# A gated cross-attention block with a top-8 expert mix: the first chunk taken by row tiles, the router centred once, gates folded into evictions, Newton's step on GpSimd, and a new order for the end

## The chip, the cores and the metric

The kernel runs on one core of a Trainium2 chip. The metric is the device time of one execution in microseconds (us). Beside the times of several runs there is one profiled execution, from which all rows below come. A core has five engines with instruction streams of their own: TensorE (PE in the profile; its weight loads are PEld), VectorE (DVE), ScalarE (ACT), GpSimd (POOL) and SyncE (SP, which only issues DMA transfers; ACT issues some too). An engine works through its stream in order and waits on semaphores for what others produce. TensorE writes to PSUM[...]; DVE and ACT carry results from there to SBUF, which all engines share.

## The reference, cut to what matters

The input `x` is 8 batches of 512 rows by 2048 columns, float32; `c` has the same shape. Per batch:

```python
h   = layernorm(x)                       # over the 2048 columns of each row
q   = Wq @ h + bq ; k = Wk @ h + bk      # 256 x 2048, in patches of 128 columns
val = Wv @ c + bv
s   = q_head.T @ k_head / sqrt(32)       # 8 heads, 128 x 128 in each patch, masked
o   = gelu(softmax(s) @ val_head)
x1  = x + tanh(g_xattn) * (Wo @ o + bo) * mask
h2  = layernorm(x1)
p   = softmax(h2 @ Wr.T + br)            # 64 experts for each row of 2048 columns
w   = the 8 largest of p, zeros elsewhere
out = x1 + tanh(g_ffn) * (h2 * sum(w) + w @ Eb)
```

Wq, Wk and Wv are 256 x 512, Wo is 512 x 256, Wr and Eb are 64 x 2048. A row of a batch (512 of them, four tiles of 128) is a token for the router.

## The kernel before, in words

**Tiles and steps.** A batch is cut into 4 chunks of 512 columns, so there are 32 chunks (`ch` 0 to 31; the last is `z`), each 512 rows in four row tiles (`m` 0 to 3). A step `g` of the main loop is half a chunk, two patches of 128 columns: 64 steps, of which 62 are in the loop (L755 to L940) and the last two, with all that is left over, in an end written out by hand (L943 to L1050). A batch is 8 steps.

**What a step does.** `scores(g)` puts q·k into the four score banks of PSUM (sc0 to sc3); `maxima` (L459, DVE), `exps` (L468, ACT, 16 instructions) and `divide` (L476 DVE, L477 POOL) make the softmax; `turn` (L491, PE) and `turned` (L497, ACT) transpose it, one step later; `weigh` (L510) multiplies it with the values, two steps later. For the next chunk `queries_and_keys` (L361 to L405) computes half of q and k by seven block products in place of eight, with sums of inputs and outputs on DVE and POOL: the sum u4 (L392, POOL) is read by ks (L400, DVE), which frees a PSUM buffer. These products, the values (L415) and others share two PSUM buffers ("mm"); transposes share two others ("tr"). `attend` (PE L539, DVE L545, POOL L548) projects a finished chunk and adds it to x in `xr`; `statistics2` (L558), `turn_x` (L563, L565) and `logits` (L574) feed the second norm and the router. When a batch is done, `gather` (L598), `choose` (L605), `choose_exps`, `select` (L630) and `turn_weights` (L653) find the eight experts of each token, and 12 steps later `scale_x` (L674 POOL, in the end L672 ACT too) and `mix` (PE L685, DVE L689, output DMA L690) make the output in eight parts of two row tiles each.

**The norms.** Statistics are collected in pieces by DVE (L264, L558). `aggregate` merges them (L244), adds epsilon (L245, DVE) and takes a power on POOL (L246); `refine` (L251 to L255) is one Newton step for the inverse square root, on DVE. For the first norm of the next batch both are called in the step with `g % 8 == 5`: `aggregate` ahead of the first divide, `refine` behind `queries_and_keys`. For the second norm they are called in the step `fin == 2` (the third step of the next batch). `norm` (L273) then applies it; in the loop ACT does (L285), in the prologue DVE and POOL (L290).

**The prologue** (L698 to L748). The loads of the first batch's x are spread over the SP and ACT queues. PE first computes values(0,0), (0,1) and (1,0), then the first chunk's q and k (pf, L344) in two halves of two row tiles each, as `norm` delivers them; sums of weights are on POOL (L208 to L210).

**The router's mean.** Logits are taken of x1 without its norm. `choose` puts the norm in afterwards, with the column sums of the router's weights (`rwsum`, made in `router_sums` by 32 PE passes at g = 1, L747), by two DVE operations for each row tile (L609, L613). The two tanh gates scale Wo (L936, POOL, g = 1) and the expert biases (L938, POOL, g = 3).

**Order.** Nothing is reordered by a scheduler: each engine executes its instructions in the order in which the program names them. A DMA goes out when its engine comes to it; eight completion slots are used in turn over the program's DMAs.

Of the kernel before, what the change touches and what calls it, by code (L numbers as in the profile page):

```python
# [16 lines left out]
P = 128  # L17
# [18 lines left out]
def flamingo_gated_kernel(  # L36
# [81 lines left out]
    def load_mask(ch):  # L118
        t = work.tile([P, CW], F32, tag="mk", name=f"mk_{ch}", bufs=4)
        nc.sync.dma_start(t, masks[ch // NCH, :, columns(ch)].to_broadcast([P, CW]))  # L120
        mks[ch] = t
# [33 lines left out]
    load_first_x(0)  # L155
    load_cx(0, 1)
    nc.scalar.dma_start(bv_sb, bv.partition_broadcast(P))
    load_first_x(1)

    def load_projections():  # L160
        nc.sync.dma_start(wq_sb, wqT.rearrange("(m p) e -> p m e", p=P))
        nc.scalar.dma_start(wk_sb, wkT.rearrange("(m p) e -> p m e", p=P))
        load_first_x(2)
        load_first_x(3)
        with nc.allow_non_contiguous_dma(reason="short bias vectors onto partitions"):
            nc.scalar.dma_start(bq_sb, bq.rearrange("(t p) -> p t", p=P))
            nc.scalar.dma_start(bk_sb, bk.rearrange("(t p) -> p t", p=P))
            nc.scalar.dma_start(bo_sb, bo.rearrange("(t p) -> p t", p=P))
        nc.scalar.dma_start(gates[:, 0:1], g_xattn.partition_broadcast(P))
        nc.scalar.dma_start(gates[:, 1:2], g_ffn.partition_broadcast(P))  # L170
        nc.scalar.dma_start(rb_sb, rb.partition_broadcast(P))
        load_mask(0)
# [16 lines left out]
    nc.vector.memset(ones, 1.0)  # L189
# [17 lines left out]
    def weight_sums():  # L207
        nc.gpsimd.tensor_tensor(ws1, w21, w22, ALU.add)  # L208
        nc.gpsimd.tensor_tensor(ws2, ws1, w11, ALU.subtract)
        nc.gpsimd.tensor_tensor(ws4, w12, ws2, ALU.subtract)  # L210
# [20 lines left out]
    def aggregate(st, n, name, m0=0, m1=NM):  # L231
# [9 lines left out]
        mv, v, r = lns[name][:3]  # L241
# [3 lines left out]
        nc.vector.tensor_scalar(v[:, ms], mv[:, ms, 1], EPS, None, ALU.add)  # L245
        nc.gpsimd.tensor_tensor(r[:, ms], v[:, ms], half[:, ms], ALU.pow)  # L246

    def refine(name, m0=0, m1=NM):
        mv, v, r, y, nmean = lns[name]
        ms = slice(m0, m1)  # L250
        nc.vector.tensor_tensor(y[:, ms], r[:, ms], r[:, ms], ALU.mult)  # L251
        nc.vector.tensor_tensor(y[:, ms], y[:, ms], v[:, ms], ALU.mult)
        nc.vector.tensor_scalar(y[:, ms], y[:, ms], -0.5, 1.5, ALU.mult, ALU.add)
        nc.vector.tensor_tensor(r[:, ms], r[:, ms], y[:, ms], ALU.mult)
        nc.vector.tensor_scalar(nmean[:, ms], mv[:, ms, 0], -1.0, None, ALU.mult)  # L255
        if m1 == NM:
            del lns[name]
        return nmean, r
# [14 lines left out]
    def norm(ch, ms=range(NM), engines=None):  # L273
        nmean, rs = ln1[ch // NCH]
        if ch // NCH not in nmrs and not engines:
            nmr = small.tile([P, NM], F32, tag="nmr", name=f"nmr_{ch}")
            nc.vector.tensor_tensor(nmr, nmean, rs, ALU.mult)
            nmrs[ch // NCH] = nmr
# [3 lines left out]
        for m in ms:  # L282
            e = engines[m % 2] if engines else nc.scalar
            if e is nc.scalar:
                e.activation(  # L285
                    xn[ch][:, m, :], source[:, m, :], AF.Identity,
                    bias=nmrs[ch // NCH][:, m : m + 1], scale=rs[:, m : m + 1],
                )
                continue
            e.tensor_scalar(  # L290
# [45 lines left out]
    def first_queries_and_keys():  # L336
# [4 lines left out]
        for m0 in range(0, NM, 2):  # L341
            for i, (w, e, pt) in enumerate(parts):
# [5 lines left out]
                if m0 == 0:  # L348
                    continue
# [359 lines left out]
    for i in range(NPP):  # L709
        values(0, 1, i)  # L710
# [374 lines left out]
```

## Time and profile before

| | |
|---|---|
| median of 3 runs | 1371.03 us (1370.95 to 1373.88) |
| the profiled execution | 1372.72 us |
| its span (first to last instruction) | 1370.9 us |
| PE busy, and idle in the span | 1317.3 us, 53.6 us |
| DVE, ACT, POOL busy | 912.9, 832.0, 778.0 us |
| first product of chunk 0 (pf) begins, ends | 26.67 us, 40.57 us |
| one batch of the steady part | 161.96 us |
| first scores of the end | 1274.65 us |
| first add of the last batch's output | 1355.79 us |

A group of the profile's rows reads: line, engine, operation, output <- input, partitions x elements, count, busy time, mean ns. A row of the timeline reads: start, duration, engine, line, operation, output <- input, count, and in brackets the idle time before it and what ended that. A row by stretches gives its length, the busy time (and number of instructions) of PE, PEld, DVE, ACT and POOL, then the granted clock of TensorE (1.00 is full), the DMA engines' share and GB/s. Engine names with a q (SPq, ACTq) are issues of DMAs.

### The profile page before, as it was taken

How to read it: one execution, taken by the hardware profiler on the slowest of the kernel's cores; microseconds unless marked ns; L12 is line 12 of the kernel's file. 1: busy time of each engine (PE TensorE's matmuls, PEld its weight loads, DVE VectorE, ACT ScalarE, POOL GpSimd, SP SyncE). 2: the span in 40 equal slices, each digit the busy share in tenths (PEclk: the TensorE clock that was granted, in tenths of full speed). 3: DMA queues.
4: the chain of work that ended last, by engine and by line, in shares of the span. 5: the costliest groups of instructions: out<-in, count | busy, mean ns of one | idle time of the engine just before them, and what ended most of it. 6: DMA issues, size and time to landing. Idle time of an engine off the chain costs nothing.

```text
span 1370.9 us, 26555 instructions
## 1 busy us (share of the span) xinstructions
PE 1317.3 (96%) x9816; PEld 961.0 (70%) x9816; DVE 912.9 (67%) x1981; ACT 832.0 (61%) x2837; POOL 778.0 (57%) x656
## 2 busy tenths in 40 slices
PE   7899999999999999999999999999999999999984
PEld 4686777777777677767777777776777777776642
DVE  5556665676676766786667767677677766567536
ACT  0565666757656666747665675666675566575533
POOL 3456565555566655557555566655556665556452
PEclk9999999999999999999999999999999999999997
DMA  8432323424434433444442444343444343232213
GB/s 276 133 102 71 101 65 129 131 70 156 153 131 139 161 100 133 147 140 141 151 137 96 146 162 141 129 158 97 139 147 161 109 131 105 75 122 78 104 67 123
DMA packets 109666, 173.32 MB, mean 126 GB/s; under 512 B 9185, under 2 KB 43617, under 8 KB 109409
## 3 DMA queue, kind: packets, MB, share of 16 engines
q1 hardware_dynamic: 105680, 168.32, 37.5%
q10 hardware_dynamic: 3856, 3.32, 0.7%
q8 instruction: 77, 1.26, 0.4%
q14 instruction: 53, 0.43, 0.1%
HBM read 138.06 MB, written 33.55 MB: 125 GB/s over the span
## 4 chain that ended last, share of the span: by engine, by line
PE 84%; DVE 11%; POOL 2%; DMA 1%; issue 1%; ACT 0%; DVEq 0%; POOLq 0%; ACTq 0%
PE qk L378 27%; PE po L539 16%; PE pv L415 13%; PE pt L491 7%; PE pl L574 4%; PE pb L685 4%; PE pa L510 4%; PE sc L447 3%; PE px L563 3%; DVE st L558 3%; DVE st L264 2%; PE sc L438 1%; PE pf L344 1%; DMA cx<-in_ctx 1%; DVE ks L405 1%
## 5 line engine op out<-in xcount | busy, mean ns | idle before, releaser
L477 POOL TENSOR_TENSOR at<-at,rsum 128x1024 f32<-128x1024 f32 x128 | 244.3, 1909 | 289.9 <-DVE rsum L476 255.4
L468 ACT ACTIVATE at<-sc,nmx 128x128 f32<-128x128 f32 x1024 | 365.7, 415 | 16.1 <-DVE nmx L459 16.1
L468 ACT ACTIVATION_READ_ACCUMULATOR at<-sc,nmx 128x1 f32 x1024 | 260.1, 254 | 0.0
L415 PE MATMUL pv<-wv_sb,cx 128*128 128x256 f32 x1024 | 242.6, 386 | 10.2 <-DMA cx<-in_ctx 10.2
L539 PE MATMUL po<-o,wo_sb 128*128 128x512 f32 x512 | 233.8, 599 | 0.0
L415 PEld LDWEIGHTS pv<-wv_sb,cx 128*128 128x128 f32 x1024 | 191.4, 194 | 33.8 <-DMA cx<-in_ctx 10.6
L548 POOL TENSOR_TENSOR xr<-t,xr 128x512 f32<-128x512 f32 x128 | 165.9, 1296 | 79.9 <-DVE t L545 79.5
L497 ACT COPY atT<-pt 128x512 f32<-128x512 f32 x256 | 151.1, 623 | 60.4 <-PE pt L491 60.3
L520 ACT COPY o<-pa 128x512 f32<-128x512 f32 x64 | 37.6, 587 | 243.9 <-PE pa L510 243.9
L459 DVE TENSOR_REDUCE nmx<-sc 128x4 f32<-128x512 f32 x256 | 158.7, 681 | 16.7 <-PE sc L447 16.6
L545 DVE SCALAR_TENSOR_TENSOR t<-po,bo_sb,mk 128x512 f32<-128x512 f32 x128 | 96.1, 751 | 109.5 <-PE po L539 104.6
L491 PEld LDWEIGHTS pt<-ident,at 128*128 128x128 f32 x1024 | 123.3, 142 | 61.8 <-issue 41.5
L539 PEld LDWEIGHTS po<-o,wo_sb 128*128 128x128 f32 x512 | 94.3, 190 | 100.4 <-issue 93.9
L565 ACT COPY x1T<-px 128x512 f32<-128x512 f32 x128 | 74.9, 587 | 139.3 <-PE px L563 136.2
L491 PE MATMUL pt<-ident,at 128*128 128x128 f32 x1024 | 152.2, 277 | 5.8 <-POOL at L477 5.3
L378 PE MATMUL qk<-xt,wq_sb 128*128 128x256 f32 x496 | 129.6, 384 | 4.0 <-DVE u L386 3.9
L378 PE MATMUL qk<-xn,ws 128*128 128x256 f32 x496 | 128.6, 382 | 0.0
L378 PE MATMUL qk<-xn,wk_sb 128*128 128x256 f32 x496 | 127.5, 380 | 0.0
L689 DVE TENSOR_TENSOR xr<-pb,xr 128x512 f32<-128x512 f32 x128 | 81.8, 683 | 36.4 <-PE pb L685 33.4
L674 POOL TENSOR_SCALAR xr<-xr,xa,xd 128x512 f32<-128x512 f32 x120 | 94.4, 798 | 18.6 <-DVE xa L650 18.6
L378 PEld LDWEIGHTS qk<-xn,ws 128*128 128x128 f32 x496 | 94.7, 191 | 13.0
L378 PEld LDWEIGHTS qk<-xn,wk_sb 128*128 128x128 f32 x496 | 89.4, 190 | 9.7
(108 smaller groups left out, 2016.3 us busy)
## 6 DMA issues: line engine op xcount, KB each, us to landing
out_dram<-xr SPq DMA_DIRECT2D x64, 512.0 KB, 3.4
cx<-in_ctx SPq DMA_DIRECT2D x63, 512.0 KB, 5.2
raw<-in_x SPq DMA_DIRECT2D x112, 256.0 KB, 3.4
xn<-in_x SPq DMA_DIRECT2D x28, 1024.0 KB, 7.3
xr<-in_x SPq DMA_DIRECT2D x28, 1024.0 KB, 7.8
mk<-in_mask_Bx1x_ff SPq DMA_DIRECT2D x32, 256.0 KB, 5.3
xr<-in_x SPq DMA_DIRECT2D x8, 256.0 KB, 6.4
xr<-in_x ACTq DMA_DIRECT2D x8, 256.0 KB, 6.9
```

Of the source, the lines that this page charges most:

```text
L378: nc.tensor.matmul(out_, w_[:, j, es], xb[:, j, :], start=(j == 0), stop=(j == NM // 2 - 1))
L415: nc.tensor.matmul(pv[:, i, :], cx[:, m, i * W : (i + 1) * W], wv_sb[:, m, :], start=(m == 0), stop=(m == NM - 1),)
L459: nc.vector.tensor_reduce(p["nmx"][:, r, :, :], p["sc"][r], AX.X, ALU.max, negate=True)
L468: nc.scalar.activation(p["at"][i][:, h, :], p["sc"][r][:, i, e, :], AF.Exp, bias=p["nmx"][:, r, i, e : e + 1], accum_out=p["rsum"][:, i, h ...
L477: (engine or nc.gpsimd).tensor_tensor(p["at"][i], p["at"][i], rs[:, :, None].to_broadcast([P, H, W]), ALU.mult)
L491: nc.tensor.transpose(pt[:, r, :], p["at"][i][:, e * HR + r, :], ident)
L497: nc.scalar.copy(p["atT"][i][:, e * HR : (e + 1) * HR, :], p.pop("pt"))
L539: nc.tensor.matmul(po[:, cs], wo_sb[:, e, m * P : (m + 1) * P], os_[ch][:, e, cs], start=(e == 0), stop=(e == NE - 1),)
L545: nc.vector.scalar_tensor_tensor(t[:, cs], po[:, cs], bo_sb[:, m : m + 1], mks[ch][:, cs], ALU.add, ALU.mult)
L548: nc.gpsimd.tensor_tensor(xc, t[:, cs], xc, ALU.add)
L674: nc.gpsimd.tensor_scalar(xc, xc, a, d, ALU.mult, ALU.add)
L689: nc.vector.tensor_tensor(xc, pb[i], xc, ALU.add)
```

## The change

1. **First chunk.** The x rows are loaded first, with Wq, Wk and cx(0,1) ahead of rows 1 to 3; mask 0, the short vectors, the gates and the router bias follow on ACT's queue; cx(1,0) and mask 1 stand behind them on SP's. The prologue runs over single row tiles: statistics, `aggregate`, the norm of chunks 0 and 1 (all on ACT), and that tile's four products; values(0,1) come after the first tile, values(1,0) in step 0. The sums of weights go from POOL to DVE, behind the last tile.
2. **Norms.** `refine` is merged into `aggregate`, all small operations behind the merge are on POOL, and so is the product of mean and inverse deviation (`shares_of_mean`). In the steps with `g % 8 == 5` the whole stands behind the first divide and ahead of `queries_and_keys`.
3. **Router.** In place of `router_sums` and the first of `choose`'s two operations, `centre_router` (at the end of g = 3) subtracts from the router's weights their mean over the columns.
4. **Gates.** Wo is scaled on ACT; the expert biases are no longer scaled, but the transposed weights are, as they are carried out of PSUM.
5. **Select.** The four small operations on `a` and `d` go from DVE to POOL, and the sum they need stands earlier.
6. **First statistics of batch 1.** The extra pieces in the steps 0 to 2 are read at the end of the step instead of behind the maxima.
7. **The end** has a new order: the last scores earlier, `scale_x` in pairs, parts 4 to 7 of the last but one batch's mix later, the adds of `attend(z)` on DVE, the last chunk turned by row tiles (`turn_last`), mixes held in PSUM until their adds, rows split between ACT and POOL in the last `scale_x`, the last two outputs split over two queues.

```diff
+    nc.sync.dma_start(wq_sb, wqT.rearrange("(m p) e -> p m e", p=P))
+    nc.scalar.dma_start(wk_sb, wkT.rearrange("(m p) e -> p m e", p=P))
     load_cx(0, 1)
+    for m in range(1, NM):
+        load_first_x(m)
+    load_mask(0, nc.scalar)
+    with nc.allow_non_contiguous_dma(reason="short bias vectors onto partitions"):
+        nc.scalar.dma_start(bq_sb, bq.rearrange("(t p) -> p t", p=P))
+        nc.scalar.dma_start(bk_sb, bk.rearrange("(t p) -> p t", p=P))
+        nc.scalar.dma_start(bo_sb, bo.rearrange("(t p) -> p t", p=P))
     nc.scalar.dma_start(bv_sb, bv.partition_broadcast(P))
...
+    nc.scalar.dma_start(gates[:, 0:1], g_xattn.partition_broadcast(P))
+    nc.scalar.dma_start(gates[:, 1:2], g_ffn.partition_broadcast(P))
+    nc.scalar.dma_start(rb_sb, rb.partition_broadcast(P))
+    load_cx(1, 0)
+    load_mask(1)
...
-    nc.vector.memset(ones, 1.0)
+    nc.vector.memset(ones, 1.0 / S)
...
     def weight_sums():
-        nc.gpsimd.tensor_tensor(ws1, w21, w22, ALU.add)
...
+        nc.vector.tensor_tensor(ws1, w21, w22, ALU.add)
...
-        nc.vector.tensor_scalar(v[:, ms], mv[:, ms, 1], EPS, None, ALU.add)
-        nc.gpsimd.tensor_tensor(r[:, ms], v[:, ms], half[:, ms], ALU.pow)
-
-    def refine(name, m0=0, m1=NM):
...
+        e = nc.gpsimd
+        e.tensor_scalar(v[:, ms], mv[:, ms, 1], EPS, None, ALU.add)
+        e.tensor_tensor(r[:, ms], v[:, ms], half[:, ms], ALU.pow)
+        e.tensor_tensor(y[:, ms], r[:, ms], r[:, ms], ALU.mult)
+        e.tensor_tensor(y[:, ms], y[:, ms], v[:, ms], ALU.mult)
+        e.tensor_scalar(y[:, ms], y[:, ms], -0.5, 1.5, ALU.mult, ALU.add)
+        e.tensor_tensor(r[:, ms], r[:, ms], y[:, ms], ALU.mult)
+        e.tensor_scalar(nmean[:, ms], mv[:, ms, 0], -1.0, None, ALU.mult)
...
+    def shares_of_mean(b, ms=slice(0, NM)):
...
+        nc.gpsimd.tensor_tensor(nmrs[b][:, ms], nmean[:, ms], rs[:, ms], ALU.mult)
...
-        for m in range(NM):
-            nc.vector.scalar_tensor_tensor(
-                lg[:, m, :], rwsum, nmean[:, m : m + 1], lg[:, m, :], ALU.mult, ALU.add
-            )
...
+        a = small.tile([P, NM], F32, tag="xa", name=f"xa_{b}")
+        d = small.tile([P, NM], F32, tag="xd", name=f"xd_{b}")
+        nc.vector.tensor_reduce(a, top, AX.X, ALU.add)
...
+        nc.gpsimd.tensor_tensor(a, a, t["rs"], ALU.mult)
+        nc.gpsimd.tensor_scalar_mul(a, a, tgates[:, 1:2])
+        nc.gpsimd.tensor_tensor(d, a, t["nmean"], ALU.mult)
+        nc.gpsimd.tensor_scalar(a, a, 1.0, None, ALU.add)
...
-        nc.scalar.copy(wT, pw)
+
+        nc.scalar.activation(wT, pw, AF.Copy, scale=tgates[:, 1:2])
...
+    new_queries_and_keys(0)
+    for m in range(NM):
+        for j in range(NCH):
+            statistics(0, m, j, xr[j][:, m, :])
+        ln1[0] = aggregate(st1[0], S // 512, "1_0", m, m + 1)
+        shares_of_mean(0, slice(m, m + 1))
+        norm(0, (m,))
+        norm(1, (m,))
+        if m == NM - 1:
+            mask(0)
+        next(projections)
+        if m == 0:
+            for i in range(NPP):
+                values(0, 1, i)
+    st1.pop(0)
+    weight_sums()
+    values_out(0, 0)
+    values_out(0, 1)
+    for k in range(3):
+        sums_of_x(1, k)
+    weight_sums_in_place()
...
+    def centre_router():
+
+        nc.vector.tensor_reduce(rwsum, rw_sb.rearrange("p k e -> p e k"), AX.X, ALU.add)
         pr = ps_tr.tile([P, E], F32, tag="tr", name="pr")
...
+        nc.tensor.matmul(pr, ones, rwsum, start=True, stop=True)
+        nc.vector.tensor_tensor(
+            rw_sb, rw_sb, pr[:, None, :].to_broadcast([P, NK, E]), ALU.subtract
+        )
...
-            if fin == 5 and b4 + 2 < B:
-                aggregate(st1.pop(b4 + 2), S // 512, f"1_{b4 + 2}")
...
             divide(g, 0)
+            b1 = g // SPB + 1
+            if g % SPB == 5 and b1 < B:
+                ln1[b1] = aggregate(st1.pop(b1), S // 512, f"1_{b1}")
+                shares_of_mean(b1)
...
-            router_sums()
-            nc.gpsimd.tensor_scalar_mul(wo_sb, wo_sb, tgates[:, 0:1])
+            nc.scalar.activation(wo_sb, wo_sb, AF.Copy, scale=tgates[:, 0:1])
         if g == 3:
-            nc.gpsimd.tensor_scalar_mul(eb_sb, eb_sb, tgates[:, 1:2])
+            centre_router()
+        read_x(len(pieces))
...
+    scores(g)
+    weigh(h0 - 1)
+    weighed(h0 - 1)
+    maxima(g, (0, 1))
+    maxima(g, (2, 3))
+    mix(b - 1, 2)
+    for k in (4, 5):
+        scale_x(b - 1, k)
+    turn_x(z - 2, 0)
...
+    for m in (0, 1):
+        attend(z, m, engine=nc.vector, tag=t_raw)
         statistics2(z - 1, m)
         statistics2(z, m)
...
+    turn_last(0)
+    turn_last(1)
+    logits(z - 1)
+    logits_out(z - 1)
+    turn_last(2)
+    mix(b - 1, 5)
+    turn_last(3)
...
+    mix(b - 1, 6, hold=True)
     choose(b)
     choose_exps(b)
+    added(b - 1, 6)
...
     for k in range(2 * NCH):
-        scale_x(b, k, k % 2 == 0)
+        scale_x(b, k, (0,), nc.scalar)
+        scale_x(b, k, (1,))
     for k in range(2 * NCH):
-        mix(b, k)
+        mix(b, k, hold=True)
+        added(b, k, (nc.sync, nc.scalar) if k >= 2 * NCH - 2 else (nc.sync,))
```

## The prediction

> **What bounds the kernel now.** I read the page first (engine shares and the 40 slices), then busy time by stretches, then the timeline wherever TensorE (PE) has idle time, then the groups of GpSimd (POOL).
>
> ```profile
> PE 1317.3 (96%) x9816; PEld 961.0 (70%) x9816; DVE 912.9 (67%) x1981; ACT 832.0 (61%) x2837; POOL 778.0 (57%) x656
> PE   7899999999999999999999999999999999999984
> PEclk9999999999999999999999999999999999999997
> ```
>
> PE is busy 96% of the span; the other engines have a third to spare. The lower digits of PE stand at the two ends only, and there alone the granted clock falls. The same by stretches (length, then busy time with instruction count of PE, PEld, DVE, ACT, POOL, then granted clock, DMA share, GB/s):
>
> ```profile
> 0.00:27.00 27.00, 16.84 (x49) 13.45 (x50) 14.99 (x43) 1.28 (x1) 6.25 (x11) 0.87 0.94 298
> 27.00:41.00 14.00, 13.89 (x35) 5.80 (x34) 5.31 (x17) 3.50 (x6) 8.66 (x8) 1.00 0.83 216
> 290.00:1250.00 960.00, 955.04 (x7244) 703.15 (x7240) 664.78 (x1429) 618.31 (x2117) 577.55 (x488) 1.00 0.41 133
> 1274.60:1325.30 50.70, 43.81 (x355) 26.95 (x353) 22.29 (x37) 25.45 (x87) 24.19 (x23) 0.93 0.29 105
> 1325.30:1370.90 45.60, 28.30 (x108) 14.09 (x106) 26.80 (x71) 13.81 (x28) 13.25 (x14) 0.81 0.28 104
> ```
>
> From 290 to 1250 us PE idles 5.0 us in 960: work taken from another engine there is worth almost nothing, and work put in front of PE costs in full. Of the 53.6 us that PE idles (1370.9 − 1317.3), 10.2 lie in the first 27 us, 24.2 in the last 96.3. So the change is decided at the ends, and by whether it breaks the middle.
>
> **Start: +6.5 us.** Before, the products of the first chunk (pf, L344) run from 26.67 to 40.57 us. The start of the timeline, PE beside the queues:
>
> ```profile
> 20.29 6.55 PE L415 MATMUL pv<-wv_sb,cx 128*128 128x256 f32 x16 [3.78 <-DMA cx<-in_ctx]
> 21.92 0.42 ACTq L168 DMA_DIRECT2D bo_sb<-in_L_xattn_bo  x1
> 23.45 0.41 ACTq L171 DMA_DIRECT2D rb_sb<-in_L_ffn_router_bias  x1
> 23.89 1.28 ACT L285 ACT_TABLE_LOAD   x1 [23.89 <-DMA xr<-in_x]
> ```
>
> The bo issue waits until 21.92: wq, the issue eight places earlier in program order, left at 13.50 and took 8.4 us to land. The other waits of these two queues that I followed fit the same spacing of eight. Now all norms of chunk 0 are on ScalarE (ACT), and 18 issues stand on its queue ahead of the first. The last, rb, stands eight behind the new place of cx(1,0) on SyncE's queue (SP). That in turn stands eight behind a piece of row 2 that I put down as landed at 16.6 (the DMAs move 367 GB/s from 5 to 20 us, and only what lies ahead of it counts). 16.6 + 8.2 for cx(1,0) under load = 24.8 for rb; + .41 issue, + 1.28 table load, + .75 for one ACT norm = 27.25 for the first operand of PE. The four rows' products are 4 × 3.43 = 13.7, and values(0,1), now between them, 3.46. PE has then been idle since about 13 us. [...] the row, 16 pv matmuls at 6.55 after 3.78 idle where the 16 at 622.51 take 3.62, loses 2.9 to 3.1. I take 2.6. End of pf: 27.25 + 17.2 + 2.6 = 47.05, against 40.57: +6.5 (+4 to +8.5: whether the wait resolves at 22.5 or 26.5). Hidden: x rows landing earlier, since ACT isn't there to use them.
>
> **First steps: −1.3 us in sum.** After pf, DVE has ks, three weight sums (.68 each, from POOL), two vT (.69), w21 and bo before the maxima, which come 5.1 us after pf (before: 2.0); scores cover part, and values(1,0), 16 matmuls of 3.46 us moved out of the prologue, stand against the router sums' 32 matmuls (pr, 3.68) that go. With the clock's dip from this stall I take +.7 (0 to +3). The extra row statistics go ahead of later maxima in g = 2 and 3: +.7. The new centring at g = 3 puts a DVE reduce over 128 × 1024 (1.3: twice the .68 of 128 × 512), one matmul and a DVE subtract over as much (1.2) in front of DVE's next maxima: +1.5 (0 to +3); the four DVE operations saved per batch (.87) have PE as their cover and count nothing. Against it stands a stall that goes. GpSimd's eb_sb scaling (5.44 us, L938) held the adds that PE turns next:
>
> ```profile
> 115.67 0.33 PE L563 MATMUL px<-ident,xr 128*128 128x128 f32 x1 [1.39 <-POOL xr L548]
> 117.08 0.33 PE L563 MATMUL px<-ident,xr 128*128 128x128 f32 x1 [1.08 <-POOL xr L548]
> 118.11 1.82 PE L378 MATMUL qk<-xn,ws 128*128 128x256 f32 x4
> ```
>
> Waits of 1.39 + 1.08 and, behind them, three groups at low clock (1.82 and two more, against their full-clock 1.03; together 1.76): −4.2. It becomes a scale inside an eviction, at nothing (ACT, the same copy). The wo_sb scaling goes from POOL (2.85) to ACT at g = 1, hidden under ACT's idle third. Sum .7 + .7 + 1.5 − 4.2 = −1.3.
>
> **Middle: +2.5 us.** Newton's step, five DVE operations of .16 per batch and norm, becomes a chain of eight on POOL, each waiting for the one before. Once per batch (g mod 8 = 5, seven times) it stands between divide(g,0) and the u4 add of queries_and_keys. Rows there: what POOL does now, and who waits for u4.
>
> ```profile
> L246 POOL TENSOR_TENSOR rs<-v,half 128x4 f32<-128x4 f32 x15 | 15.4, 1024 | 75.2 <-DVE v L245 75.2
> L392 POOL TENSOR_TENSOR u<-u,s 128x256 f32<-128x256 f32 x62 | 45.0, 726 | 30.2 <-DVE s L391 30.1
> 621.50 0.73 POOL L392 TENSOR_TENSOR u<-u,s 128x256 f32<-128x256 f32 x1
> 622.26 0.48 DVE L400 SCALAR_TENSOR_TENSOR ks<-qk,bk_sb,u 128x256 f32<-128x256 f32 x1 [0.81 <-POOL u L392]
> ```
>
> No small POOL arithmetic is in the trace. POOL's adds cost .73 for 256 columns and 1.28 for 512 (L308), so a straight line leaves .2 at none: 7 × (.2 + .09 for the wait) + 1.02 for pow = 3.0. POOL runs its scale_x and divide earlier, since pow no longer stands ahead of them, and u4 begins at 621.85 instead of 621.50. The ks after it holds a PSUM buffer that PE's next product wants: .35 × 7 = 2.5. Bounds: 0 (the step in PE's slack) and 10 (each operation .16 dearer). At LN2 (fin = 2) the same chain has 3.8 us before the next divide; it is hidden. The four operations of select (a, d) end at 607.9 by the same price, against 608.09 for their user: hidden, barely.
>
> **End: −14.3 us.** The end, as the timeline has it before:
>
> ```profile
> 1304.26 6.04 POOL L674 TENSOR_SCALAR xr<-xr,xa,xd 128x512 f32<-128x512 f32 x8
> 1312.21 1.97 PE L491 MATMUL pt<-ident,at 128*128 128x128 f32 x8 [4.53 <-POOL at L477]
> 1343.84 1.97 PE L598 MATMUL pg<-ident,lgT 128*128 128x64 f32 x8 [2.58 <-DVE lgT L588]
> 1352.48 0.69 PE L659 MATMUL pw<-ident,rest 128*128 128x128 f32 x2 [6.67 <-DVE rest L642]
> 1355.79 1.29 DVE L689 TENSOR_TENSOR xr<-pb,xr 128x512 f32<-128x512 f32 x2 [2.41 <-PE pb L685]
> ```
>
> From the first scores of the end (1274.65, called 0): last scores +20, the eight scalings delay divide(g,1) and PE 4.5, first output projection of the last chunk (attend(z,0)) +50.6, gather +69.2, first output add +81.1, end +96.25. After: scores(g) come ahead of four turns, weigh and turn_x, at +11; attend(z,0) at +39.9: three of the six mixes ahead of it move behind (1.2 of PE each, 3.6), the 4.5 goes, and the waits of scores for DVE's t (2.6 in this stretch by the view of waits) go with their buffers' new order. From there to gather it was 18.6, of which PE worked 15.8 and idled 2.8, almost all before gather, for lgT behind the statistics on DVE. Now the statistics lie between the adds: 15.8 + 1.2 for one mix moved in + .7 for DVE's lgT add = 17.7, gather +57.6. From gather to first add it was 11.9; off come the four DVE operations of choose (.9), five of select (.8), and .9 because pg (1.97 for eight small matmuls) finds PE warm: first add +66.9. From first add to end it was 15.1, four megabytes of output at 371 to 389 GB/s, and stays: end +82.0, −14.3 (−10: one stall like the old one; −19: the adds of the held mixes early and nothing waiting). The last outputs, split over two queues, save nothing while the DMAs are full.
>
> **Sum.** +6.5 − 1.3 + 2.5 − 14.3 = −6.6. The profiled execution took 1372.7 us (span 1370.9 and 1.8 around it), so 1366.1; the median of the runs is 1.7 lower, so 1364.4 there. I predict 1364.
>
> **Rivals.** A: the ACT queue isn't held. For it: the spacing of eight is inferred from waits that fit it. Norms then follow the rows (the last at about 30 us, pf end 34), 12.5 earlier than in my sum: 1352. B, slower: small POOL operations are dear. At .29 with its wait each one the stall is .35; at .6 the chain takes 5.2, the stall 2.5 plus as much for PE at lower clock behind it, 7 × 5 = 35 less what slack recovers, say half: +17 in place of 2.5: 1379. It decides from about .48 per operation, where the stall of 1.7 each time eats what is in hand. For it: nothing of that size is in the trace; against it: the straight line, and a POOL pow on 128 × 2 at .72 and on 128 × 4 at 1.02, more than half of it by element. C: the end's new order stalls elsewhere (one row of statistics on DVE ahead of an add, PSUM buffers shared by held mixes) and gives 8 only: 1364 + 6.3 = 1370 to 1371, no change. That the change does nothing isn't possible: the order of all engines moves.
>
> **How the numbers follow.** Mine .64 (own range 1357 to 1370, from the bounds above taken as half independent), A .13, B .12, C .11. Runs of this kernel tell apart 0.2%, 2.7 us, so faster is below 1368.3 and slower above 1373.8. Faster: .58 + .13 + .03 of C = .74; same: .06 + .06 = .12; slower: B .12 + .02 of C = .14. The range 1354 to 1375 leaves out most of A below and most of B above.
>
> **What would show it.** Right: first pf at 27 to 28 us behind ACT's rb issue, pf end near 47; no PE wait at 115 to 121; PE stalls under .5 at u4 of g = 5, 13, 21; POOL's small operations at .2; from first scores of the end to the last 82 us. Wrong: pf near 15 us (A); PE idle of over 1.5 at each g = 5 mod 8, or clock below 1.00 there (B); more than 86 us of end (C).

## The result

The changed kernel takes 1361.65 us (median; 1361.33 to 1364.93) against 1371.09 for the kernel before, measured beside it; the ratio is 0.9932 (95% interval 0.9912 to 0.9952), so it is faster by 9.4 us. Its profiled execution took 1361.84 us, with a span of 1360.0 against 1370.9. The forecast was 1364, faster. The total came near partly by luck: its terms were wrong by up to 5.8 us, and not all in the same direction, as the anchors show. Here is when TensorE (PE) reaches the same piece of work in the two traces:

| PE begins | before, us | after, us | after − before | change since the row above |
|---|---|---|---|---|
| scores, step 0 (pf has ended) | 40.50 | 46.21 | +5.71 | +5.71 |
| scores, step 1 | 50.77 | 62.71 | +11.94 | +6.23 |
| scores, step 3 | 85.52 | 91.95 | +6.43 | −5.51 |
| scores, step 4 | 102.91 | 112.48 | +9.57 | +3.14 |
| scores, step 10 | 224.21 | 229.88 | +5.67 | −3.90 |
| scores, step 60 | 1237.08 | 1239.43 | +2.35 | −3.32 |
| scores, step 62 (the end's first) | 1274.65 | 1275.67 | +1.02 | −1.33 |
| scores, step 63 | 1294.65 | 1286.73 | −7.92 | −8.94 |
| first projection of the last chunk | 1325.29 | 1315.98 | −9.31 | −1.39 |
| gather (pg) | 1343.84 | 1333.76 | −10.08 | −0.77 |
| first add of the last output (DVE) | 1355.79 | 1344.47 | −11.32 | −1.24 |
| last instruction | 1370.90 | 1360.00 | −10.90 | +0.42 |

So the start costs 5.7 (forecast +6.5), the first steps come to nothing (−1.3), the middle gains 3.3 (forecast a loss of 2.5), two steps ahead of the end gain another 1.3 (nothing), and the end gains 11.9 (−14.3).

The page of the changed kernel, busy time and slices: PE's low digit at the start is lower than before, the one at the end higher.

```profile
PE 1305.5 (96%) x9786; PEld 951.3 (70%) x9786; DVE 886.3 (65%) x1814; ACT 835.7 (61%) x2843; POOL 791.8 (58%) x802
PE   3899999999999999999999999999999999999996
PEclk7999999999999999999999999999999999999997
```

The start of its timeline, the ACT queue beside ACT and PE:

```profile
24.46 0.44 ACTq L169 DMA_DIRECT2D rb_sb<-in_L_ffn_router_bias  x1
24.94 1.28 ACT L281 ACT_TABLE_LOAD   x1 [24.94 <-DMA bk_sb<-in_L_xattn_bk]
...
26.23 5.75 ACT L281 ACTIVATE xn<-xr,nmr,rs 128x512 f32<-128x512 f32 x8
...
27.10 3.71 PE L336 MATMUL pf<-xn,wq_sb 128*128 128x512 f32 x4 [14.95 <-ACT xn L281]
30.64 1.88 PE L336 MATMUL pf<-xn,wk_sb 128*128 128x512 f32 x4
```

ACT doesn't begin before the last of its DMA issues has left: that of rb starts at 24.46 and takes 0.44, and the table load starts at 24.94. The first row tile had been ready for it since about 14 us: the last small operation on its statistics (nmr, POOL) began at 13.81. The first four products take twice what the next four take (3.71 for 1.88; the granted clock is 0.50 from 27.10 to 30.64 us and 1.00 from there to 32.36).

The step g = 29, where Newton's chain stands ahead of u4 on POOL:

```profile
626.04 0.20 POOL L273 TENSOR_TENSOR nmr<-nmean,rs 128x4 f32<-128x4 f32 x1
626.19 0.73 POOL L384 TENSOR_TENSOR u<-u,s 128x256 f32<-128x256 f32 x1
626.57 0.60 PE L407 MATMUL pv<-wv_sb,cx 128*128 128x256 f32 x2
626.95 0.48 DVE L392 SCALAR_TENSOR_TENSOR ks<-qk,bk_sb,u 128x256 f32<-128x256 f32 x1 [1.44 <-POOL u L384]
```

u4 begins 11.68 us after this step's scores (11.35 before), and ks waits for it 1.44 (0.81 before). PE has no gap: it goes on with pv while ks waits.

The end by stretches: from the first scores of the end to the first projection of the last chunk, to gather, to the first output add, to the last instruction (length, then busy time and count of PE, PEld, DVE, ACT, POOL, granted clock, DMA share, GB/s):

```profile
1275.67:1315.98 40.31, 37.96 (x342) 24.00 (x340) 18.11 (x31) 27.00 (x89) 21.08 (x19) 1.00 0.26 93
1315.98:1333.76 17.78, 16.07 (x71) 7.67 (x69) 14.97 (x26) 4.39 (x8) 6.91 (x12) 1.00 0.16 59
1333.76:1344.47 10.71, 7.68 (x24) 3.49 (x26) 6.28 (x25) 4.50 (x14) 4.18 (x9) 0.69 0.26 99
1344.47:1360.00 15.53, 8.28 (x28) 3.38 (x26) 9.84 (x16) 3.41 (x5) 3.01 (x5) 0.72 0.72 271
```

Before, the first stretch was 50.64 with clock 0.93; now it is 40.31 at 1.00. The last two still have a slow clock (0.69 and 0.72).

### The profile page after: what moved, and what is told of

Its sections match the earlier page's. It is cut to its first block, busy times and chain, and to the rows that moved or that the text cites. A ratio compares the mean times of both kernels' runs of the same rounds, so it can differ in the third digit from the quotient of the medians.

```text
span 1360.0 us, 26464 instructions
## 1 busy us (share of the span) xinstructions
PE 1305.5 (96%) x9786; PEld 951.3 (70%) x9786; DVE 886.3 (65%) x1814; ACT 835.7 (61%) x2843; POOL 791.8 (58%) x802
## 4 chain that ended last, share of the span: by engine, by line
PE 89%; DVE 5%; DMA 2%; ACT 2%; POOL 1%; issue 1%; DVEq 0%; ACTq 0%
PE qk L370 27%; PE po L531 17%; PE pv L407 13%; PE pt L483 8%; PE pb L677 5%; PE pa L502 5%; PE pl L566 4%; PE sc L439 4%; PE px L555 3%; PE sc L430 2%; PE pf L336 1%; DMA cx<-in_ctx 1%; POOL at L469 1%; ACT at L460 1%; DVE st L550 1%
## 5 line engine op out<-in xcount | busy, mean ns | idle before, releaser
L407 PE MATMUL pv<-wv_sb,cx 128*128 128x256 f32 x1024 | 238.6, 381 | 7.3 <-DMA cx<-in_ctx 6.8
L540 POOL TENSOR_TENSOR xr<-t,xr 128x512 f32<-128x512 f32 x124 | 160.5, 1294 | 90.9 <-DVE t L537 90.5
L407 PEld LDWEIGHTS pv<-wv_sb,cx 128*128 128x128 f32 x1024 | 188.6, 191 | 30.1 <-DMA cx<-in_ctx 6.8
L370 PEld LDWEIGHTS qk<-xn,wk_sb 128*128 128x128 f32 x496 | 89.4, 190 | 11.2 <-issue 1.6
```

The costliest lines, as they stand in the source:

```text
L370: nc.tensor.matmul(out_, w_[:, j, es], xb[:, j, :], start=(j == 0), stop=(j == NM // 2 - 1))
L407: nc.tensor.matmul(pv[:, i, :], cx[:, m, i * W : (i + 1) * W], wv_sb[:, m, :], start=(m == 0), stop=(m == NM - 1),)
L540: (engine or nc.gpsimd).tensor_tensor(xc, t[:, cs], xc, ALU.add)
```

## The experiments

All of them change the changed kernel. Where only the trace is used, it is of one execution. A stretch of low clock that one trace has and another has not moves all that follows, so shifts are taken between two steps; where no such stretch lies between, they repeat from trace to trace to some hundredths of a microsecond (from step 10 to step 60 six of the variants below, which leave these steps alone, differ from the changed kernel by 0.01 or less), so tenths can be read.

### The short loads off ACT's queue

```diff
-    load_mask(0, nc.scalar)
+    load_mask(0)
...
-        nc.scalar.dma_start(bq_sb, bq.rearrange("(t p) -> p t", p=P))
+        nc.sync.dma_start(bq_sb, bq.rearrange("(t p) -> p t", p=P))
...
-    nc.scalar.dma_start(rb_sb, rb.partition_broadcast(P))
+    nc.sync.dma_start(rb_sb, rb.partition_broadcast(P))
```

The issues of bk, bo, bv and the two gates move in the same way.

> Theory (ACT is held by its own DMA queue): the last issue that ACT makes ahead of its first norm is then a piece of x, near 15.6 us; first norm near 17, first pf near 18, the last row's pf ends between 34 and 37 us (changed kernel: 46.3), and all later steps are earlier by as much: 1350 to 1353 us. Rival (the rows of x, or a cold TensorE, set the end of pf): pf still ends after 44 us, and the time stays within 2 us of the changed kernel's 1361.7.

Measured: 1352.6 us, 0.9878 (0.9855 to 0.9900) of the kernel before. Its timeline:

```profile
15.53 1.28 ACT L281 ACT_TABLE_LOAD   x1 [15.53 <-DMA xr<-in_x]
16.83 1.52 ACT L281 ACTIVATE xn<-xr,nmr,rs 128x512 f32<-128x512 f32 x2
17.69 3.78 PE L336 MATMUL pf<-xn,wq_sb 128*128 128x512 f32 x4 [5.17 <-ACT xn L281]
...
35.23 1.88 PE L336 MATMUL pf<-xn,wk_sb 128*128 128x512 f32 x4
```

ACT, the first norm and the first product come 9.4 us earlier, and the whole kernel 9.1. The hold of ACT by its own DMA queue is shown. The gain is smaller than the 12.5 of the forecast's rival A: from 23.19 on PE works without a gap until pf ends at 37.1, with the last row's norm done at 29.7, so the products, and no longer the rows, set the end of pf.

### The old end

The end is that of the kernel before, line for line, with `scale_x` and `aggregate` called in their new form; all else as changed.

> Theory (the gain of the end is its order): with the end written as before, all else as changed, the stretch from the first scores of the end to the last instruction is 96 us again (within 1.5; changed kernel 84.3), and the time 1372 to 1375 us. Rival (much of the gain comes from the lighter DVE and the gates in the evictions, whatever the order): that stretch is 90 us or less, the time below 1368.

Measured: 1375.06 us, 1.0036 (1.0026 to 1.0046) of the kernel before. From the first scores of the end (1277.87) to its last instruction (1373.4) it takes 95.5 us, against 84.3 with the new end and 96.25 before. So the order of the end carries 11.2 of its 11.9 us. The rest of the change, without the new end, makes the kernel slower by 0.4%. Of the 13.4 us that this kernel takes more than the changed one, 1.65 arise in step 0, where the products behind a wait are slow (the first four take 2.07 for the changed kernel's 1.13; last section).

### One block of scalings

In the kernel before, eight `scale_x` instructions (6.04 us of POOL) stood ahead of the last divide and PE waited 4.53 us. The prediction named these scalings as the delay and let the 4.5 go with the new end, which spreads them. This undoes only the spreading:

```diff
-    for k in (4, 5):
-        scale_x(b - 1, k)
     turn_x(z - 2, 0)
...
+    for k in (4, 5, 6, 7):
+        scale_x(b - 1, k)
     exps(g, 3)
     divide(g, 1)
...
-    for k in (6, 7):
-        scale_x(b - 1, k)
     mix(b - 1, 4)
```

> In the new end, the four late scale_x pairs stand in one block ahead of the last divide again, as before. Theory (spreading them takes the stall of 4.5 us away): GpSimd is busy 6 us there, the last divide is late, TensorE waits 4 to 5 us for it and the end takes 88 to 90 us from its first scores in place of 84.3. Rival (other order of the end covers it): less than 1.5 us more.

Measured: 1361.83 us, span 1360.0, the same as the changed kernel in every anchor. So in the new end it isn't the spreading that takes the 4.5 away. A second kernel has the block and also moves the last turns back to where they stood, ahead of the logits:

```diff
+    turn_(g, 0, 1)
     gelu(z - 1)
+    turn_(g, 2, 3)
     logits(z - 2)
     logits_out(z - 2)
...
-    turn_(g, 0, 1)
...
-    turn_(g, 2, 3)
```

> The late scalings in one block ahead of the last divide, and besides the last turns right behind weigh and before the logits, as they stood before the change. Theory (either of the two was enough to take the stall of 4.5 us away; one block alone cost nothing because the turns come later): TensorE waits 3 to 4.5 us for the last divide, the first projection of the last chunk and the end come 3 to 5 us later than in the changed kernel. Rival (the block never mattered): less than 1.5 us.

Measured: span 1365.9. Of its 5.9 us more, 2.2 had come ahead of the end, so the end takes 3.6 more, within the 3 to 5 expected. Two rows of the kernel with the block alone, where the turn finds the divide (ended at 1305.83) long done:

```profile
1303.93 1.90 POOL L469 TENSOR_TENSOR at<-at,rsum 128x1024 f32<-128x1024 f32 x1
...
1309.14 1.04 PE L483 MATMUL pt<-ident,at 128*128 128x128 f32 x8
```

and the same two with the turns moved back as well, with what follows on PE:

```profile
1306.15 1.89 POOL L469 TENSOR_TENSOR at<-at,rsum 128x1024 f32<-128x1024 f32 x1
1308.10 1.09 PE L483 MATMUL pt<-ident,at 128*128 128x128 f32 x8 [1.99 <-POOL at L469]
1309.12 3.59 PE L566 MATMUL pl<-x1T,rw_sb 128*64 128x512 f32 x8
```

PE waits 1.99 us, not the 3 to 4.5 expected, and the eight logits behind it take 3.59 where they take 1.94 in the changed kernel. Together that is the 3.6. With the turns late the block costs nothing, with the turns early it costs 3.6: the later turns alone would have done. Whether the spread pairs alone would have done too, no run shows.

### Eight more operations on POOL

```diff
-        nc.gpsimd.tensor_tensor(nmrs[b][:, ms], nmean[:, ms], rs[:, ms], ALU.mult)
+        for _ in range(9 if b else 1):
+            nc.gpsimd.tensor_tensor(nmrs[b][:, ms], nmean[:, ms], rs[:, ms], ALU.mult)
```

> The last small GpSimd operation of the chain (mean times deviation) is done nine times in place of once, the same result each time, in the seven steps g mod 8 = 5. Eight more at 0.28 us make u4 2.2 us later. Theory (the step that failed was that a late u4 costs TensorE what it is late; there is slack of some tenths, and it decides from there): TensorE stalls by 1 to 2.2 us in each of the seven, the scores of step 60 come 8 to 16 us later, or up to 25 with low clock behind the stalls. Rival (u4 has room of more than 2 us): less than 2 us over all seven.

Measured: from step 5 to step 60 nothing at all (scores shifted by 0.36 at step 5 and by 0.35 at step 60). The rival was right. The same place in its trace (the nine operations, then u4, and what PE does):

```profile
626.40 2.41 POOL L274 TENSOR_TENSOR nmr<-nmean,rs 128x4 f32<-128x4 f32 x9
...
626.93 3.62 PE L408 MATMUL pv<-wv_sb,cx 128*128 128x256 f32 x16
...
628.76 0.73 POOL L385 TENSOR_TENSOR u<-u,s 128x256 f32<-128x256 f32 x1
...
629.53 0.48 DVE L393 SCALAR_TENSOR_TENSOR ks<-qk,bk_sb,u 128x256 f32<-128x256 f32 x1 [3.65 <-POOL u L385]
630.39 1.88 PE L532 MATMUL po<-o,wo_sb 128*128 128x512 f32 x4
```

ks waits 3.65 us and PE still has work: the values write to the score bank sc0 and the two projections behind them to sc1 and sc2. Neither needs the buffer that ks frees. Eight operations more at 0.28 are as if each of the chain's eight took 0.56, more than the 0.48 from which rival B of the prediction was to decide. The span of 1362.8 is longer by 2.8 us, but 2.7 of that arise between the scores of steps 60 and 62, where the turn, the mix and the scores behind PE's wait take 1.06, 2.08 and 1.92 for the changed kernel's 0.60, 1.13 and 1.06 (last section).

### Newton's step on DVE

First at its new place:

```diff
-        e = nc.gpsimd
+        first = name == "1_0"
+        e = nc.gpsimd if first else nc.vector
...
-        e.tensor_tensor(r[:, ms], v[:, ms], half[:, ms], ALU.pow)
+        nc.gpsimd.tensor_tensor(r[:, ms], v[:, ms], half[:, ms], ALU.pow)
...
-        nc.gpsimd.tensor_tensor(nmrs[b][:, ms], nmean[:, ms], rs[:, ms], ALU.mult)
+        (nc.vector if b else nc.gpsimd).tensor_tensor(nmrs[b][:, ms], nmean[:, ms], rs[:, ms], ALU.mult)
```

> Theory (the 0.37 us that the step g mod 8 = 3 gains in each batch comes from Newton's step leaving DVE at the second norm): with Newton's step and the product of mean and deviation back on DVE in the loop, logits waits for DVE again by 0.3 us in each such step, and the scores of step 60 come 2 to 2.6 us later than in the changed kernel. Rival (it comes from the four operations taken out of choose): no such wait, scores of step 60 within 0.4 us.

Measured: 1423.2 us, 61 more than the changed kernel; both readings missed it. The step g = 29 of its trace:

```profile
647.92 1.90 POOL L470 TENSOR_TENSOR at<-at,rsum 128x1024 f32<-128x1024 f32 x1 [5.78 <-DVE rsum L469]
648.29 1.54 DVE L246 TENSOR_SCALAR v<-mv 128x4 f32<-128x4 f32 x1
649.92 1.04 POOL L247 TENSOR_TENSOR rs<-v,half 128x4 f32<-128x4 f32 x1
650.99 0.16 DVE L248 TENSOR_TENSOR y<-rs 128x4 f32<-128x4 f32 x1 [1.15 <-POOL rs L247]
...
652.40 0.42 DVE L379 TENSOR_TENSOR u<-qk,s 128x256 f32<-128x256 f32 x1
652.88 1.86 PE L371 MATMUL qk<-xt,wq_sb 128*128 128x256 f32 x4 [3.00 <-DVE u L379]
```

DVE stands still for POOL's divide and pow, ahead of the sums of `queries_and_keys`, and those do free the buffer that PE wants next: 3.00 us of stall, and the two groups of four products behind it take 1.86 and 1.91 for the changed kernel's 1.03. With a second stall at the other norm this makes 9.1 us per batch in the steady part. It undid more than was meant, so it doesn't answer the question; it shows that at the new place the chain has to be on POOL, where nobody but POOL waits for it. The operation v takes 1.54 and ends at 649.83, the divide at 649.82; of the eleven v between 290 and 1250 us the shortest takes 0.17 and the median 1.54. What lengthens it, no run shows.

Then as before, in two parts and at the old places, which answers it:

> Newton's step in the loop as in the kernel before: on DVE, in two parts, at its old places; the first batch's and all else as changed. Theory (the 0.37 us that the step g mod 8 = 3 gains is DVE's relief at the second norm): logits waits 0.3 us in each such step and the scores of step 60 come 2 to 2.6 us later. Rival (it is the four operations fewer in choose, or both are needed): less than 0.7 us. Both expect no stall like that of the version with DVE waiting for GpSimd at the new place.

Measured: scores shifted by 2.22 us at step 10 (1.69 of it from step 0, where two groups of four products behind a wait take 1.99 and 1.89 for the changed kernel's 1.13 and 1.03; last section) and by 4.27 at step 60. Between them lie 2.05, in portions of 0.25 at step 10 and 0.35 to 0.37 at each later step g mod 8 = 3, exactly where the changed kernel had gained them. The waits of PE between 290 and 1250 us, this kernel's row first, then that of the kernel before:

```profile
PE pl L573 <- DVE xr L694: 1.4, 5, 0.3
```

```profile
PE pl L574 <- DVE xr L689: 3.2, 10, 0.3
```

The five waits of 0.3 at the second norm are back; the changed kernel has none. Newton's step on DVE had held the output adds, which hold the buffer of the next logits.

### The router's part

The first undoes the four small operations of `select`:

```diff
-        nc.gpsimd.tensor_tensor(a, a, t["rs"], ALU.mult)
+        nc.vector.tensor_tensor(a, a, t["rs"], ALU.mult)
```

and its three followers in the same way.

> Theory (the 0.31 us that the step g mod 8 = 5 gains comes from select's four small operations leaving DVE): with these four back on DVE, logits waits for DVE by 0.3 us in each such step, scores of step 60 2 to 2.4 us later. Rival (the gain there comes from Newton's step of the first norm leaving DVE, or from the sum standing earlier): no such wait, scores of step 60 within 0.4 us.

Measured: from step 10 to step 60 later by 0.29 us, no wait of logits for DVE. The second undoes those, the centring and the operations saved in `choose`:

```diff
-        nc.vector.tensor_reduce(rwsum, rw_sb.rearrange("p k e -> p e k"), AX.X, ALU.add)
...
-        nc.tensor.matmul(pr, ones, rwsum, start=True, stop=True)
+        for k in range(NK):
+            nc.tensor.matmul(pr, ones, rw_sb[:, k, :], start=(k == 0), stop=(k == NK - 1))
+        nc.scalar.copy(rwsum, pr)
...
+            nc.vector.scalar_tensor_tensor(
+                lg[:, m, :], rwsum, nmean[:, m : m + 1], lg[:, m, :], ALU.mult, ALU.add
+            )
```

> The router's column sums by 32 passes at step 1, choose's four extra operations, and select's four small ones on DVE, all as before; the rest as changed. Theory: from step 3 to 4 the 3.1 us of the centring go (scores of step 4 no later than those of step 3 by more than 0.5 against the kernel before), from step 1 to 2 about 3.5 us come back, and in each batch DVE is late again by enough for logits to wait 0.3 us in the step g mod 8 = 5 (scores of step 60 later by 2 us beside what the first steps leave). Rival (DVE work there is covered in the new order whatever is added): no such wait, less than 0.7 us over all batches.

Measured: from step 1 to 2 later by 2.78, from 3 to 4 earlier by 3.14 and from 4 to 5 by another 0.69, from step 10 to 60 later by 0.25 only. The first part of the theory held roughly (2.78 for about 3.5, 3.14 for 3.1), the second fell. The 0.69 is low clock behind PE's wait, which in the changed kernel reaches into step 4 (0.59 from 112.14 to 116.30 us; rows in the next experiment). So centring the router once costs 3.83 and saves 2.78, 1.05 us net at the front, and gives at most 0.3 in the body. The saved DVE operations were covered.

### The sum of the router's weights a step earlier

```diff
+        if g == 2:
+            sum_router()
         if g == 3:
             centre_router()
```

> The strided sum of the centring (1.88 us on DVE) at the end of step 2, the matmul and the subtraction at the end of step 3 as in the changed kernel. Theory (TensorE's wait of 2.74 us for that sum, and 0.9 us of low clock behind it, are its place and not its work): scores of step 4 come 2.5 to 3.2 us earlier against those of step 2. Rival (the sum is as much in the way at step 2, because the maxima of step 3 stand behind it): less than 1 us earlier.

What it moves, in the changed kernel's timeline at the turn from step 3 to 4:

```profile
110.11 1.88 DVE L732 TENSOR_REDUCE rwsum<-rw_sb 128x64 f32<-128x1024 f32 x1
112.14 0.41 PE L734 MATMUL pr<-rwsum,ones 128*128 128x64 f32 x2 [2.74 <-DVE rwsum L732]
112.48 0.61 PE L430 MATMUL sc<-mneg,negw 32*128 32x512 bf16 x4
112.87 1.93 PE L439 MATMUL sc<-ks,qs 32*128 32x128 f32 x32
```

Measured: against those of step 2, the scores of step 4 come earlier by 2.13, short of the 2.5 expected, and those of step 5 by 2.99, since the low clock lay behind the begin of step 4's scores; 1359.23 us in the one execution. PE no longer waits for the sum, and its scores take 1.27 behind it where they took 1.93. Of the 3.83 that the centring cost, 2.99 were its place and not its work.

### TensorE kept busy while the experts are chosen

```diff
     mix(b - 1, 6, hold=True)
+    warm = ps_tr.tile([P, P], F32, tag="tr", name="warm")
+
+    def keep_warm(n):
+        for _ in range(n):
+            nc.tensor.transpose(warm, ident, ident)
+
+    keep_warm(10)
...
     mix(b - 1, 7, hold=True)
+    keep_warm(20)
     select(b)
```

> Thirty transposes of the identity into a PSUM tile that nobody reads (10 behind the held mix 6, 20 behind the held mix 7) keep TensorE busy while the experts are chosen. Theory (the slow first mixes behind the weights are low clock: first add 2.2 us after the weights): clock 1.00 through the last mixes, first add of the last batch 1 to 1.3 us earlier, the end 0.8 to 2 us earlier: 1360 to 1361. Rival (outputs leave at the rate of the DMAs anyway, or the clock does not follow such filling): end within 0.5 us.

Measured: 1359.96 us, 0.9928 (0.9912 to 0.9945) of the kernel before, beside which it ran. From the first scores of the end to the last instruction it takes 82.7 us against 84.3. The last mixes in the changed kernel, then with PE kept busy:

```profile
1342.30 10.45 PE L677 MATMUL pb<-eb_sb,wT 64*128 64x512 f32 x32 [0.56 <-ACT wT L651]
1344.47 1.29 DVE L687 TENSOR_TENSOR xr<-pb,xr 128x512 f32<-128x512 f32 x2 [2.28 <-ACT xr L662]
```

```profile
1341.91 8.46 PE L677 MATMUL pb<-eb_sb,wT 64*128 64x512 f32 x32 [0.56 <-ACT wT L651]
1343.12 9.66 DVE L687 TENSOR_TENSOR xr<-pb,xr 128x512 f32<-128x512 f32 x16 [1.21 <-ACT xr L662]
```

The granted clock from 1343 to 1348 us is 1.00 where it was 0.50; the first add follows the first mix by 1.21 instead of 2.17. The 1.6 us are the end's, in the traces; the ratios to the kernel before, 0.9928 and the changed kernel's 0.9932, have intervals that overlap and don't tell the two apart.

### Together

The short loads on SP, the early sum, PE kept busy, and besides:

```diff
+        if m == 1:
+            weight_sums()
         if m == NM - 1:
+            values_out(0, 0)
+            values_out(0, 1)
             mask(0)
...
-    weight_sums()
-    values_out(0, 0)
-    values_out(0, 1)
```

> The changed kernel with the short loads on SP (its run: -9.1 us), the strided sum at step 2 (-2.9), TensorE kept busy while the experts are chosen (-1.6), and besides the sums of weights on DVE behind the second row tile and the two evictions of the values ahead of the last mask, so that behind the last row's product DVE has 3.4 us less ahead of the first maxima and TensorE's waits there (1.48 for the eviction, 2.06 for u) shrink. Theory (the four are independent, and the last gives 2 to 3): 1361.7 - 13.6 - 2.5 = 1345.6, 1344 to 1348 us; pf ends near 37, scores of step 1 come 2 to 3 us earlier against those of step 0. Rival (DVE's work moved ahead delays a row's norm, or a stall freed at one place turns up at the next): 1349 or more.

Measured: 1346.69 us (1346.40 to 1347.18), 0.9823 (0.9810 to 0.9837) of the kernel before: 24.3 us less than that, 15 less than the changed kernel. pf ends at 36.7 and PE's wait of 1.48 for the eviction is gone; scores of step 1 come 13.9 us after those of step 0, against 16.5 in the changed kernel. Of what the parts promised, 1.6 were lost again between steps 60 and 62, where the mix behind PE's wait takes 1.96 for 1.13 and the scores behind it 1.67 for 1.06 (last section).

## Why the prediction was right, and where it wasn't

The direction came from two terms that held, start and end; the three between were each off, one of them in sign.

**Start, +6.5: right, +5.7.** ACT is held until rb has left (24.46; forecast 24.8), first pf at 27.10 (27.25). That it met so well is partly luck: cx(1,0), for which the forecast had rb wait, left at 18.05 and not 16.6, and took 6.3 and not 8.2. The size of the slow start was an error: pf and the values between take 19.1 for 17.2, so 1.9 lost, nearly all of it in the first four products (3.71 for 1.88). The row of the kernel before gave 2.9 to 3.1; the 2.6 that was taken was the author's estimate.

**First steps, −1.3: −0.04.** Up to step 3 the sum came out as forecast (+0.72 for 0.7), but by luck. The maxima of step 0 came as late behind pf as forecast (4.8 us, for 5.1); what failed is the cover. Beyond the 3.46 of values(1,0), step 0 grew by 2.8: PE waited 1.48, 2.06 and 0.78 in it, against 1.66 before. Moving DVE's work ahead took 2.6 of this back (the last experiment). Step 1 gave 1.9 beyond the 3.6 of the router sums, which no term had. The kernel before, in its step 1:

```profile
57.22 0.69 DVE L264 BATCH_NORM_STATS2 st<-raw 128x6 f32<-128x512 f32 x1 [0.46 <-DMA raw<-in_x]
58.82 1.13 PE L378 MATMUL qk<-xt,wq_sb 128*128 128x256 f32 x4 [2.28 <-DVE u L386]
59.79 1.52 PE L378 MATMUL qk<-xn,ws 128*128 128x256 f32 x4
```

Statistics stood ahead of PE's sum u on DVE, and low clock followed PE's wait (0.65 from 58.82 to 63.63 us); in the changed kernel these statistics stand at the end of the step, the wait is 1.12 and the clock behind it 1.00 (69.60 to 77.57 us). No run tests this by itself. The extra row statistics cost nothing (+0.7 forecast): step 2 adds no shift. The centring cost 3.83 for 1.5: the sum took 1.88 and not 1.3, and that PE's own product stands behind it, with a wait of 2.74 and then a clock of 0.59, was left out of the working. The stall that went with the scaling of the expert biases was worth −4.6 for −4.2: the −3.89 from step 4 to 5 contain +0.69 of the centring's low clock.

**Middle, +2.5: −3.3.** Here two steps failed. "The ks after it holds a PSUM buffer that PE's next product wants" was wrong. POOL's small operations cost .20 each and .28 from one to the next, the chain was as long as forecast, and u4 was 0.33 late for the forecast 0.35; but PE asks for that buffer only after the values and two projections, and even 2.5 us late costs it nothing. With that, rival B's break-even of .48 per operation had no ground (the run with eight more passed it). And DVE's relief was counted at nothing, with PE as its cover. For choose that was right. For Newton's step at the second norm it wasn't: 2.05 us, shown. The other 1.27 of the middle appear as +0.10 in the steps g mod 8 = 4 (12, 20 and so on) and −0.31 in the next. The +0.10 fits the eviction with the gate in it, 0.47 for 0.37, for which PE waits. The −0.31 matches five other waits of logits for DVE's output adds that the kernel before has, 0.34 each, in the steps g mod 8 = 5. None of the three runs that undo Newton's step, select, or select and choose brings these back; which part of the change took them away stays open.

**End, −14.3: −11.9, a matter of size.** To the gather the sum held: scores at +11.06 (forecast +11), the first projection at +40.3 (+39.9), gather at +58.1 (+57.6). Two of its terms did not. The 4.5 did not hang on spreading the scalings, as the later turns would have hidden them. And the 2.6 for waits of scores on DVE's t was not there to be gained: it is the sum of five waits over the whole kernel before, and none of them lies in this stretch. About as much went by the clock, which no term had: PE's busy time in the stretch fell by 5.8 (43.75 to 37.96), of which the three mixes are 3.2, while the granted clock rose from 0.93 to 1.00. Most of that stood behind the old stall, where turn and weigh took 1.97 and 1.94, at a clock of 0.50 (1312.21 to 1316.20 us), for 1.09 and 1.08 at full clock. From gather to first add the forecast was 9.35, measured 10.71. Two terms of this held or nearly (pg at full clock .9 for .9, choose .7 for .9). The failing term is "five of select (.8)": before, rest ended at 1352.42 and the turn of the weights began at 1352.48, while the four operations on a and d followed on DVE beside it, so they were not on the path. The sum that was moved ahead is on it now (reciprocal to end of rest 2.73, before 2.50), and the eviction with the gate in it adds 0.1. The output took 15.5 for 15.1, with clock 0.72 instead of 0.84. It was not simply bound by its transfers: with PE kept busy and its clock at 1.00 (1333.8 to 1352 us) the end gained 1.6.

**Between, 0: −1.3.** No step foresaw this. Both kernels wait for the experts' weights at step 60 and about as long, but behind it the clock was 0.54 in the one (1254.57 to 1258.25 us) and 1.00 in the other (1256.98 to 1259.27); this 1.3 is luck, as the last section shows. Before:

```profile
1254.57 0.48 PE L659 MATMUL pw<-ident,rest 128*128 128x128 f32 x2 [1.94 <-DVE rest L642]
1254.85 1.06 PE L491 MATMUL pt<-ident,at 128*128 128x128 f32 x4
1255.84 2.08 PE L685 MATMUL pb<-eb_sb,wT 64*128 64x512 f32 x4
```

After:

```profile
1256.98 0.44 PE L647 MATMUL pw<-ident,rest 128*128 128x128 f32 x2 [2.01 <-DVE rest L634]
1257.26 0.60 PE L483 MATMUL pt<-ident,at 128*128 128x128 f32 x4
1257.99 1.13 PE L677 MATMUL pb<-eb_sb,wT 64*128 64x512 f32 x4
```

## What to carry to other kernels

ACT, with loads to issue ahead of its first computing, began to compute when the last of them had left (24.94 us in the changed kernel, 15.53 with the short loads on SP): read an engine's queue rows before putting the first work of a kernel on it. Lateness of a result cost nothing here until the bottleneck engine asked for the buffer that its reader frees (ks waited 3.65 us for u4, and PE lost nothing), so follow the buffers by tag, not the order of the code. A stall can have two covers, and the second then earns nothing (the block of scalings cost 0.0 with the turns late, 3.6 with them early): undo each by itself before crediting it. A sum that comes out right doesn't show that its terms are: compare them one by one.

## What the runs showed of the hardware that was not expected

A pause of PE of about 2 us is followed by slow products in some of these traces and not in others, with the same work on both sides of it. At step 60 PE waits 2.00 or 2.01 us for the experts' weights in the changed kernel and in nine of its variants. Five of the nine then lost 1.4 to 2.7 us up to the scores of step 62 (the router as before 1.51, eight more on POOL 2.73, Newton's step as before 1.37, the block with the turns 1.40, together 1.61); the other four (the short loads, the block alone, the early sum, TensorE kept busy) came within 0.01 of the changed kernel, whose clock behind the wait is 1.00. In step 0 the wait for u is 2.06 in the changed kernel and in the kernel with the old end, and only the second lost, 1.65 us (the kernel with Newton's step as before lost 1.69 there in the same way). First the changed kernel, then the one with the old end:

```profile
55.62 1.13 PE L370 MATMUL qk<-xt,wq_sb 128*128 128x256 f32 x4 [2.06 <-DVE u L378]
```

```profile
56.40 2.07 PE L370 MATMUL qk<-xt,wq_sb 128*128 128x256 f32 x4 [2.06 <-DVE u L378]
```

So a difference of one to nearly three microseconds between two of these kernels can be this and nothing else.

With thirty transposes that compute nothing, 3.7 us of PE in two groups, the clock was 1.00 through a stretch of short waits (1333.8 to 1348 us; in the changed kernel 0.61 from 1335 to 1348), and in the trace the end was 1.6 us shorter.
